# Moving PSUM copies to ScalarE and elementwise steps to GpSimd in an edge-gated graph kernel

## The chip, the cores and the metric

The kernel runs on one core of a Trainium2 chip. A core has a matrix engine (TensorE, "PE" in the profile, with its weight loads under "PEld"), VectorE ("DVE"), ScalarE ("ACT"), GpSimd ("POOL") and a queue engine for transfers (SyncE, "SP"); ScalarE and GpSimd issue transfers too. Working memory is SBUF; matrix products land in PSUM. The metric is the device time of one execution in microseconds, as the median of several. A separate execution was recorded by the hardware profiler.

## The reference

The inputs are `x` of 16 x 1024 x 256 and a sparse adjacency `adj` of 1024 x 1024 (some nine nonzeros in a row). With D = 256, what is computed is

```
pre_u = x @ W1[:D];  pre_v = x @ W1[D:]
hidden[b,u,v] = relu(pre_u[b,u] + pre_v[b,v] + b1)
S[b,u,v] = sigmoid(hidden[b,u,v] @ W2 + b2)
a_t[b,v] = sum_u S[b,u,v] * adj[u,v] * x[b,u]
m_t[b,v] = (sum_u adj[u,v] * x[b,u]) * x[b,v]
z = beta1*x + beta2*(a_t @ Wa + ba) + beta3*(m_t @ Wm + bm)
```

Only the pairs (u, v) with a nonzero `adj[u,v]` matter, so the gate S is needed for edges alone. The output has the shape of `x`, in float32.

## The kernel before, in words

**Tiles.** The 16 batches go in NG = 4 groups of GB = 4, the 1024 target nodes v in NT = 8 tiles of 128. One group and one tile are a block: 32 blocks, numbered k in `order`. A block has two windows w of 64 nodes, and a window has TW = 5 slots j of 128 edges each, so a block is T = 10 steps and the whole kernel 320 steps n = 10k + s. Within a window, the edges in slot j belong to one or two quarters of 16 nodes (`QUARTERS`).

**Edge lists.** `lists(vt)`, a generator driven by the table `advance`, turns a tile of `adjT` into slots: VectorE finds the nonzeros, and `uidx`, `vidx`, `onehot` and `whose` hold, for each edge, its source node, the flat address of its weight, its target within a quarter and within a window. `fetch_val` gathers the weights themselves into `val` with GpSimd transfers, two a step while any are wanted.

**Tables.** `rows` writes h W1[:D] into `table[g]` in DRAM, whose other half is a copy of x (`copy_h`). `fetch(n)` (line 453) has GpSimd gather, for the 128 edges of step n, 128 rows of 8 KB from the table into one of NF = 5 buffers `fetched`.

**The target side.** `halves(k)` makes h W1[D:] + b1 for block k in PSUM (two halves of 128 x 512). ScalarE copies it into `X`, rounded to the matmul's fp32r format (line 418), and VectorE takes the product less `X` as `low`, the rest that rounding lost (line 419). ScalarE then puts `X` and `low` of a window into the two halves of the partitions (lines 422 and 425). Thus one fp32r matmul by a 0/1 matrix `mark` gives the sum of both parts: `expand(n)` (line 523) spreads the 128 nodes' rows over the 128 edges of step n into the PSUM tile `pc` of 128 x 1024, which has two buffers.

**A step.** `gate(n)` adds `fetched` and `pc` on VectorE into `t` in SBUF (line 539), and four `scalar_tensor_tensor` (line 543), one a batch, take the relu, multiply by W2 and sum into `sc`. ScalarE makes the sigmoid (line 546). `left_adj(n)` has already put onehot times the adj weight into the "adj columns" of the tile `left` (line 533, ScalarE); ScalarE multiplies these by the gate into the columns beside them (line 549, four a step). `aggregate(n)` (line 560) multiplies `left` by the gathered x into `acc`, both m and a at once.

**End of a block.** `half_end` copies `acc` to SBUF, `turn_over` transposes it and ScalarE writes it to `LT`; `times_h` (line 591, VectorE) multiplies its m part by h; `block_end` (line 608) multiplies by Wm and Wa into a PSUM tile `pz` that begins with the bias; `add` (line 612, VectorE) adds beta1 h in place in `h_blk`, and SyncE sends `h_blk` out. The last block has a path of its own, `tail`.

**What sets the order.** It is written out by hand: `manual_schedule` keeps each engine's queue in program order. The main loop issues, for each n: aggregate(n-1), up to two weight gathers, fetch(n+4), gate(n), left_adj(n+1), the deferred work of `do(n)`, expand(n+2), and then, at fixed s, pieces of `turn_over`, `block_end`, `halves` and `rows`. `after(step, f)` puts f into `do(step)`. So on GpSimd, fetch(n+4) stands behind the wait for aggregate(n-1), which frees its buffer. PSUM holds two tiles of `pc`, two of `acc`, and two for the small products (`small`, "misc" in the profile).

Of the kernel before, what the change touches and what calls it, by code (L numbers as in the profile page):

```python
# [13 lines left out]
P = 128  # L14
# [3 lines left out]
def kernel(  # L18
# [46 lines left out]
    GB = 4  # L65
# [292 lines left out]
    def after(step, f):  # L358
        due.setdefault(step, []).append(f)
# [48 lines left out]

    def halves(k):
        X = cuts[k] = big.tile([P, NW, GD], FR, name="X")  # L410
        low = one.tile([P, GD], FR, name="low")
        for h in range(2):
            step = yield
            c = slice(2 * h * D, (2 * h + 2) * D)
            p = small("p")
            add_row(p, b1_p)
            half_product(p, hTs[order[k]], w_v, h, True)
            nc.scalar.copy(X[:, 0, c], p)
            after(step + 1, lambda c=c, p=p: nc.vector.tensor_tensor(
                low[:, c], p, X[:, 0, c].bitcast(FP), ALU.subtract))  # L420
        yield
        nc.scalar.copy(X[W:, 1, :], X[W:, 0, :].bitcast(FP))
        for w in range(NW):
            yield
            nc.scalar.copy(X[(1 - w) * W:(2 - w) * W, w, :], low[w * W:(w + 1) * W].bitcast(FP))

    engines = mybir.EngineType
    main.enter_context(tc.manual_schedule(
# [98 lines left out]
    def left_adj(n):  # L527
        k, g, vt, w, j = where(n)
        i = vt * NW + w
        m = len(QUARTERS[j])  # L530
        o = max(2 * j - 1, 0)
        lefts[n] = wk.tile([P, 2, GB, 2, V], FP, name="left")
        nc.scalar.activation(lefts[n][:, :m, :, 0, :], onehot[:, i, o:o + m, :].unsqueeze(2).to_broadcast([P, m, GB, V]),  # L533
                             AF.Copy, scale=val[:, i, j:j + 1])

    def gate(n):
        k, g, vt, w, j = where(n)
        t = one.tile([P, GB, D], FP, name="t")
        nc.vector.tensor_tensor(t, fetched[n % NF][:, :GD].rearrange("p (b d) -> p b d", b=GB),  # L539
                                pcs.pop(n).rearrange("p (b d) -> p b d", b=GB), ALU.add)  # L540
        sc = wk.tile([P, GB], FP, name="sc")
        for b in range(GB):
            nc.vector.scalar_tensor_tensor(t[:, b, :], t[:, b, :], 0.0, w2_b,  # L543
                                           ALU.max, ALU.mult, accum_out=sc[:, b:b + 1])
        gt = wk.tile([P, GB], FP, name="gt")
        nc.scalar.activation(gt, sc, AF.Sigmoid, bias=b2_b)  # L546
        for b in range(GB):
            m = len(QUARTERS[j])
            nc.scalar.activation(lefts[n][:, :m, b, 1, :], lefts[n][:, :m, b, 0, :], AF.Copy, scale=gt[:, b:b + 1])  # L549

    def aggregate(n):
        k, g, vt, w, j = where(n)
        left, f = lefts.pop(n), fetched[n % NF]
        for i, q in enumerate(QUARTERS[j]):
            h, r = divmod(q, 2)
            first = j == h * MID and r == 0
            if first:
                accs[h] = psa.tile([P, 2, D], FP, name=f"acc{h}")
            for b in range(GB):
                nc.tensor.matmul(accs[h][b * 2 * V:(b + 1) * 2 * V, r, :],  # L560
                                 left[:, i, b].rearrange("p k v -> p (k v)"), f[:, GD + b * D:GD + (b + 1) * D],
                                 start=first, stop=(j == q + 1), skip_group_check=True)


# [5 lines left out]
    def turn_over(k, w, q, step):  # L570
# [17 lines left out]

        def times_h():
            m = LT[:, :, :, 0, v]  # L590
            nc.vector.tensor_tensor(m, m, hTs[order[k]].rearrange("p b c n -> p c b n")[:, :, :, v], ALU.mult)  # L591
            if w == NW - 1 and q == 1:
                del hTs[order[k]]
        after(step + 1, times_h)

    def block_end(k):

        g, vt = order[k]
        hb = hbs[k]
        for h in range(2):  # L600
            for bb in range(2):
                step = yield
                if bb == 0:
                    pz = small("pz")
                    add_row(pz, bias_p)
                for i, wt in enumerate((w_m, w_a)):
                    for c in range(DC):
                        nc.tensor.matmul(pz[:, bb * D:(bb + 1) * D], LTs[k][:, c, 2 * h + bb, i, :], wt[:, c, :],  # L608
                                         start=False, stop=(i == 1 and c == DC - 1), skip_group_check=True)

            def add(h=h, pz=pz):
                nc.vector.scalar_tensor_tensor(hb[:, 2 * h:2 * h + 2, :], hb[:, 2 * h:2 * h + 2, :], be1,
                                               pz.rearrange("p (b d) -> p b d", b=2), ALU.mult, ALU.add)
            after(step + 1, add)
        after(step + 2, lambda: nc.sync.dma_start(
            out[g * GB:(g + 1) * GB, vt * P:(vt + 1) * P, :].rearrange("b p d -> p b d"), hb))
        del hbs[k], LTs[k]


# [64 lines left out]
    for n in range(total + 2):  # L684
# [54 lines left out]
        elif n >= total:  # L739
# [1 line left out]
            next(end)  # L741
            go(end, n)
            go(end, n)
        if k + 1 < BS and s in (0, 2, 3, 4, 6):
            if s == 0:
                parts = halves(k + 1)
                next(parts)
# [129 lines left out]
```

## Time and profile before

| What | Value |
|---|---|
| median of 3 runs | 1183.41 us (1183.29 to 1184.95) |
| profiled execution: time, span | 1197.01 us, 1195.2 us |
| PE busy | 1097.9 us, 92% |
| DVE busy | 1066.9 us, 89% |
| ACT busy | 840.4 us, 70% |
| POOL busy | 426.1 us, 36% |
| transfers | 391.39 MB, mean 327 GB/s |
| mean granted TensorE clock | 0.973 |

The span runs from the first to the last instruction of the profiled execution; that execution is 1.1% above the median of the runs. Busy is the time in which an engine works on data; the issuing of a transfer by SP or ACT isn't counted, the gathers that GpSimd makes are. In the lists of groups a row gives line, engine, operation, output and inputs with their shapes, how many there were, and then the busy time in us, the mean time of one in ns, and the idle time of the engine just before them with what ended it. In the chain that ended last the profiler follows only the last microseconds here, so it says little.

### The profile page before, as it was taken

Reading aid. Unit: us, or ns where it says so; the run is one execution under the profiler, and the core shown is the slowest. Engines: PE = TensorE matmul, PEld = TensorE weight load, DVE = VectorE, ACT = ScalarE, POOL = GpSimd, SP = SyncE. Lnnn points to the kernel's source line nnn. Section 1 sums busy time; section 2 is a strip of 40 time slices with the busy share of each in tenths; the row PEclk is TensorE's granted clock in tenths of the full one; section 3 lists DMA queues with packets and bytes.
Section 4 is the critical chain, followed back from the end, with each engine's and each line's share of the span. In section 5 each row is a group of like instructions: output and inputs, shape, how many; then the busy total and the mean of one; then the engine's idle time right before and its main releaser. Section 6 shows DMA issues by size and latency. Waiting matters only on the chain. (4 is left out here: it accounts for less than half of the span.)

```text
span 1195.2 us, 23788 instructions
## 1 busy us (share of the span) xinstructions
PE 1097.9 (92%) x7633; PEld 724.7 (61%) x7633; DVE 1066.9 (89%) x3515; ACT 840.4 (70%) x2498; POOL 426.1 (36%) x428
## 2 busy tenths in 40 slices
PE   7667988999889898999999999999999999999986
PEld 6544655666556565666666666666666666666653
DVE  8769879989988988899899999999999999999994
ACT  3346666677667665777777777787878777777873
POOL 1557652433263226333233333333333333333330
PEclk9968899999999999999999999999999999999998
DMA  9988889899979978999999999999999999999992
GB/s 279 312 307 261 258 319 333 315 336 377 320 254 373 361 244 302 357 384 360 351 329 379 359 331 371 362 356 386 358 367 345 356 324 326 326 341 328 335 340 76
DMA packets 147046, 391.39 MB, mean 327 GB/s; under 512 B 16752, under 2 KB 105328, under 8 KB 110704
## 3 DMA queue, kind: packets, MB, share of 16 engines
q0 software_dynamic: 50016, 300.50, 68.5%
q1 hardware_dynamic: 81616, 74.99, 19.6%
q10 hardware_dynamic: 15280, 14.29, 3.7%
q8 instruction: 63, 1.03, 0.3%
q14 instruction: 71, 0.58, 0.1%
HBM read 393.78 MB, written 50.33 MB: 372 GB/s over the span
## 5 line engine op out<-in xcount | busy, mean ns | idle before, releaser
L453 POOL DMA_INDIRECT fetched<-table,uidx x320 | 329.7, 1030 | 675.5 <-PE acc L560 509.6
L543 DVE SCALAR_TENSOR_TENSOR t<-t,w_b 128x256 f32<-128x256 f32 x1280 | 469.3, 422 | 20.1 <-ACT LT L581 0.5
L539 DVE TENSOR_TENSOR t<-fetched,pc 128x1024 f32<-128x1024 f32 x320 | 388.8, 1215 | 22.4 <-DMA fetched<-table,uidx 8.6
L560 PE MATMUL acc<-fetched,left 128*32 128x256 f32 x4096 | 334.2, 394 | 32.3 <-ACT left L549 16.8
L549 ACT ACTIVATE left<-left,gt 128x32 f32<-128x32 f32 (+1 forms) x1280 | 299.4, 304 | 10.4
L523 PE MATMUL pc<-X,mark 128*128 128x512 f32 x640 | 238.1, 454 | 21.1 <-DVE t L539 13.6
L560 PEld LDWEIGHTS acc<-fetched,left 128*32 128x32 f32 x4096 | 129.9, 110 | 177.2 <-issue 46.9
L546 ACT ACTIVATE gt<-sc,b_b 128x4 f32<-128x4 f32 x320 | 95.3, 298 | 140.5 <-DVE t L543 133.9
L523 PEld LDWEIGHTS pc<-X,mark 128*128 128x128 f32 x640 | 97.2, 191 | 156.6 <-issue 102.2
L608 PE MATMUL misc<-w_a,LT 128*128 128x256 f32 x496 | 127.3, 379 | 0.0
L608 PE MATMUL misc<-w_m,LT 128*128 128x256 f32 x496 | 127.1, 378 | 0.0
L384 PE MATMUL misc<-w_u,hT 128*128 128x256 f32 x448 | 109.2, 390 | 11.0 <-ACT few L298 3.6
L533 ACT ACTIVATE left<-onehot,val 128x128 f32<-128x128 bf16 (+1 forms) x320 | 116.5, 364 | 0.0
L384 PE MATMUL misc<-w_v,hT 128*128 128x256 f32 x448 | 107.9, 384 | 0.0
L543 DVE DVE_READ_ACCUMULATOR t<-t,w_b 128x1 f32 x1280 | 104.2, 81 | 0.0
L608 PEld LDWEIGHTS misc<-w_m,LT 128*128 128x128 f32 x496 | 93.7, 189 | 17.2
L384 PEld LDWEIGHTS misc<-w_u,hT 128*128 128x128 f32 x448 | 85.8, 195 | 27.3 <-issue 4.4
L608 PEld LDWEIGHTS misc<-w_a,LT 128*128 128x128 f32 x496 | 94.2, 190 | 12.8
L568 ACT COPY ev<-acc 128x512 f32<-128x512 f32 x128 | 75.1, 587 | 34.7 <-PE acc L560 26.8
L341 POOL DMA_INDIRECT val<-in_adjT_dram,vidx x80 | 83.6, 1046 | 33.4 <-issue 21.9
L384 PEld LDWEIGHTS misc<-w_v,hT 128*128 128x128 f32 x448 | 86.7, 194 | 14.3
L581 ACT COPY LT<-misc 128x512 f32<-128x512 f32 x128 | 71.1, 575 | 24.0 <-PE pc L523 12.0
(158 smaller groups left out, 830.9 us busy)
## 6 DMA issues: line engine op xcount, KB each, us to landing
h_blk<-in_x_dram SPq DMA_DIRECT2D x31, 512.0 KB
out_dram<-h_blk SPq DMA_DIRECT2D x31, 512.0 KB
hT<-in_xT_dram SPq DMA_DIRECT2D x28, 512.0 KB
table<-tab SPq DMA_DIRECT2D x26, 512.0 KB
table<-in_x_dram ACTq DMA_DIRECT2D x24, 512.0 KB
fetched<-table,uidx POOLq DMA_INDIRECT x320
table<-in_x_dram SPq DMA_DIRECT2D x8, 512.0 KB
table<-fetched SPq DMA_DIRECT2D x6, 512.0 KB
```

The source lines that it names most:

```text
L341: nc.gpsimd.indirect_dma_start(out=val[:, i, j:j + 1], out_offset=None, in_=adj_flat, in_offset=bass.IndirectOffsetOnAxis(ap=vidx[:, i, j: ...
L384: nc.tensor.matmul(p[:, bb * D:(bb + 1) * D], hT[:, 2 * h + bb, i, :], wt[:, i, :], start=(i == 0 and not begun), stop=(i == DC - 1), skip ...
L453: nc.gpsimd.indirect_dma_start(out=fetched[n % NF], out_offset=None, in_=table[g], in_offset=bass.IndirectOffsetOnAxis(ap=uidx[:, vt * NW ...
L523: nc.tensor.matmul(pcs[n][:, c], marks[n // TW][:, j * P:(j + 1) * P], cuts[k][:, w, c], start=True, stop=True)
L533: nc.scalar.activation(lefts[n][:, :m, :, 0, :], onehot[:, i, o:o + m, :].unsqueeze(2).to_broadcast([P, m, GB, V]), AF.Copy, scale=val[:, ...
L539: nc.vector.tensor_tensor(t, fetched[n % NF][:, :GD].rearrange("p (b d) -> p b d", b=GB), pcs.pop(n).rearrange("p (b d) -> p b d", b=GB), ...
L543: nc.vector.scalar_tensor_tensor(t[:, b, :], t[:, b, :], 0.0, w2_b, ALU.max, ALU.mult, accum_out=sc[:, b:b + 1])
L546: nc.scalar.activation(gt, sc, AF.Sigmoid, bias=b2_b)
L549: nc.scalar.activation(lefts[n][:, :m, b, 1, :], lefts[n][:, :m, b, 0, :], AF.Copy, scale=gt[:, b:b + 1])
L560: nc.tensor.matmul(accs[h][b * 2 * V:(b + 1) * 2 * V, r, :], left[:, i, b].rearrange("p k v -> p (k v)"), f[:, GD + b * D:GD + (b + 1) * D ...
L568: nc.scalar.copy(evs[q], accs.pop(q))
L608: nc.tensor.matmul(pz[:, bb * D:(bb + 1) * D], LTs[k][:, c, 2 * h + bb, i, :], wt[:, c, :], start=False, stop=(i == 1 and c == DC - 1), sk ...
```

## The change

Four edits go together.

1. In `halves` both PSUM products are copied out by ScalarE: a second copy puts the product itself into `low` (now float32), and the subtraction works on SBUF alone, in place. It runs on GpSimd, except for block 0.
2. `left_adj` and `times_h` go to GpSimd (`times_h` of the last block stays on VectorE).
3. In `block_end` ScalarE copies `pz` to a new tile `z`, right after the products; GpSimd multiplies `h_blk` by beta1 in place and adds it to `z`; SyncE sends `z` out. The product by Wa comes before that by Wm.
4. `gate` has no tile `t` any more: the sum of `fetched` and `pc` is written back into `pc` in PSUM, and the four relu-and-sum instructions read and write it there.

The fourth piece of `halves` (the first copy out of `low`) moves from s = 4 to s = 5.

```diff
-        low = one.tile([P, GD], FR, name="low")
+        low = one.tile([P, GD], FP, name="low")
+        engine = nc.gpsimd if k else nc.vector
...
             nc.scalar.copy(X[:, 0, c], p)
-            after(step + 1, lambda c=c, p=p: nc.vector.tensor_tensor(
-                low[:, c], p, X[:, 0, c].bitcast(FP), ALU.subtract))
+            nc.scalar.copy(low[:, c], p)
+            after(step + 1, lambda c=c: engine.tensor_tensor(low[:, c], low[:, c], X[:, 0, c].bitcast(FP), ALU.subtract))
...
-        nc.scalar.activation(lefts[n][:, :m, :, 0, :], onehot[:, i, o:o + m, :].unsqueeze(2).to_broadcast([P, m, GB, V]),
-                             AF.Copy, scale=val[:, i, j:j + 1])
+        nc.gpsimd.tensor_scalar(lefts[n][:, :m, :, 0, :], onehot[:, i, o:o + m, :].unsqueeze(2).to_broadcast([P, m, GB, V]),
+                                val[:, i, j:j + 1], None, ALU.mult)
...
-        t = one.tile([P, GB, D], FP, name="t")
-        nc.vector.tensor_tensor(t, fetched[n % NF][:, :GD].rearrange("p (b d) -> p b d", b=GB),
-                                pcs.pop(n).rearrange("p (b d) -> p b d", b=GB), ALU.add)
+        t = pcs.pop(n).rearrange("p (b d) -> p b d", b=GB)
+        nc.vector.tensor_tensor(t, fetched[n % NF][:, :GD].rearrange("p (b d) -> p b d", b=GB), t, ALU.add)
...
-            nc.vector.tensor_tensor(m, m, hTs[order[k]].rearrange("p b c n -> p c b n")[:, :, :, v], ALU.mult)
+            (nc.vector if k == BS - 1 else nc.gpsimd).tensor_tensor(m, m, hTs[order[k]].rearrange("p b c n -> p c b n")[:, :, :, v], ALU.mult)
...
+        z = big.tile([P, GB, D], FP, name="z", bufs=1)
...
-                for i, wt in enumerate((w_m, w_a)):
+                for i, wt in ((1, w_a), (0, w_m)):
...
-            def add(h=h, pz=pz):
-                nc.vector.scalar_tensor_tensor(hb[:, 2 * h:2 * h + 2, :], hb[:, 2 * h:2 * h + 2, :], be1,
-                                               pz.rearrange("p (b d) -> p b d", b=2), ALU.mult, ALU.add)
+            sl = slice(2 * h, 2 * h + 2)
+            nc.scalar.copy(z[:, sl], pz.rearrange("p (b d) -> p b d", b=2))
+
+            def add(sl=sl):
+                nc.gpsimd.tensor_scalar(hb[:, sl], hb[:, sl], be1, None, ALU.mult)
+                nc.gpsimd.tensor_tensor(z[:, sl], hb[:, sl], z[:, sl], ALU.add)
             after(step + 1, add)
...
-            out[g * GB:(g + 1) * GB, vt * P:(vt + 1) * P, :].rearrange("b p d -> p b d"), hb))
+            out[g * GB:(g + 1) * GB, vt * P:(vt + 1) * P, :].rearrange("b p d -> p b d"), z))
...
-        if k + 1 < BS and s in (0, 2, 3, 4, 6):
+        if k + 1 < BS and s in (0, 2, 3, 5, 6):
```

## The prediction

> **What bounds the kernel now.** I began with the page's busy times, and with how they lie over the span (busy by stretches; the columns are PE, PEld, DVE, ACT, POOL, granted clock, DMA share, GB/s).
>
> ```profile
> PE 1097.9 (92%) x7633; PEld 724.7 (61%) x7633; DVE 1066.9 (89%) x3515; ACT 840.4 (70%) x2498; POOL 426.1 (36%) x428
> 300.00:360.00 60.00, 50.84 (x349) 32.50 (x350) 54.62 (x183) 39.11 (x121) 26.60 (x26) 0.97 0.86 289
> 840.00:900.00 60.00, 59.77 (x430) 39.65 (x426) 55.83 (x175) 47.20 (x143) 19.54 (x19) 1.00 1.01 366
> 1080.00:1140.00 60.00, 57.70 (x410) 36.81 (x410) 58.13 (x184) 46.94 (x146) 19.76 (x20) 1.00 0.93 331
> ```
>
> The limits differ. Late, DVE is busy 58 of 60 us and DMA 0.93; in the middle DMA is full (1.01) and PE nearly; early nothing is full, so engines wait for each other. Which of PE and DVE leads is told by the timeline of two late steps:
>
> ```profile
> 1005.41 1.22 DVE L539 TENSOR_TENSOR t<-fetched,pc 128x1024 f32<-128x1024 f32 x1
> 1006.67 0.42 DVE L543 SCALAR_TENSOR_TENSOR t<-t,w_b 128x256 f32<-128x256 f32 x1
> ...
> 1008.06 0.74 DVE L612 SCALAR_TENSOR_TENSOR h_blk<-h_blk,be,misc 128x512 f32<-128x512 f32 x1
> 1008.72 1.21 DVE L539 TENSOR_TENSOR t<-fetched,pc 128x1024 f32<-128x1024 f32 x1
> 1011.59 1.22 DVE L539 TENSOR_TENSOR t<-fetched,pc 128x1024 f32<-128x1024 f32 x1
> ```
>
> DVE goes from gate to gate with no gap. By the starts of L539, a step with the gate alone takes 2.81 us, and one with an L419, L591 or L612 besides 3.2 to 3.4. Blocks 24 to 30 take 31.1 us each: 10 x 2.81 and 3.0 for the six extras. The groups with shapes kept apart give the pieces:
>
> ```profile
> L453 POOL DMA_INDIRECT fetched<-table,uidx x320 | 329.7, 1030 | 675.5 <-PE acc L560 509.6 <-DVE t L543 52.0 <-DVE h_blk L612 44.8
> L533 ACT ACTIVATE left<-onehot,val 128x128 f32<-128x128 bf16 x192 | 74.0, 386 | 0.0
> L612 DVE SCALAR_TENSOR_TENSOR h_blk<-h_blk,be,misc 128x512 f32<-128x512 f32 x62 | 46.1, 744 | 20.7 <-PE misc L608 20.6
> L419 DVE TENSOR_TENSOR low<-misc,X 128x512 fp32r<-128x512 f32 x64 | 43.9, 686 | 19.7 <-ACT X L418 19.7
> L591 DVE TENSOR_TENSOR LT<-LT,hT 128x512 f32<-128x512 f32 x55 | 37.8, 688 | 11.1 <-ACT LT L581 10.9
> L418 ACT CAST X<-misc 128x512 fp32r<-128x512 f32 x64 | 37.3, 583 | 38.4 <-PE misc L384 32.4 <-PE pc L523 4.0 <-PE misc L578 1.6
> ```
>
> The three DVE rows that leave also carry 51.5 us of waits at the head of DVE's queue, with the next gate behind them; 37 us of these lie before 540 us.
>
> By the starts of L539 I cut the span into prologue (68.5 us), early blocks 0 to 10 (431.6), middle 11 to 22 (395.5), late 23 to 31 (278.6) and tail (21.0): 1195.2 us. The execution took 1197.0, 13.6 above the median of the runs; I take the same difference for the change.
>
> [...] L419 (PSUM) takes 686 ns, L591 (SBUF) 688.
>
> **The change part by part, per block of ten steps.**
>
> *DVE.* Two each of L612, L419 and L591 leave: 3.0 us. The gate keeps its instructions. Writing PSUM isn't in the trace; by the read rows it costs nothing[...]. I take 20 ns on the four L543s: 0.8 a block. DVE then needs 28.9 us, against 31.1.
>
> *PE* keeps its work, but expand(n+2) must now wait for the last L543 of gate(n), not for L539, some 1.4 us later. Read off the timeline where PE doesn't wait: expand 0.57 to the next start, aggregate 0.57 or 1.0 (one or two quarters), Wa and Wm products 7.4 a block, `halves` 3.9, transposes 2.0: 5.7 + 8.3 + 7.4 + 3.9 + 2.0 = 27.3 us, and 3.5 more in a block with `rows` (nine in ten in the middle), 30.5. Expand finishes 0.57 us after gate(n), and is needed after gate(n+1), 2.8 us later. So PE may lag DVE by 2.2; in steps 2 to 6 its work (16.3 us) exceeds DVE's (14.1) by just that. I cost the new wait at nothing, hidden by gate(n+1); without that cover it is up to 0.57 + 1.4 us a step. Wa ahead of Wm gives the later `times_h` 0.9 us more.
>
> *ACT* loses L533 (3.6 us) and gets four 128x512 copies (4 x 0.58): 1.3 us less. Each waits for PE at the head of its queue, where L418 waited already; the sigmoid stands behind. It has 70% load: nothing.
>
> *POOL* is where the work goes. A gather is 0.99 us and starts 1.30 apart when nothing holds it: 13.0 us. No elementwise row of POOL with these shapes exists. [...] L533's successor: [...] 0.39 by ACT's row, a gather's 0.99 as high end; I take 0.5. Sum: 10 x 0.5 + 6 x 1.2 + 2 x 0.85 = 13.9, so 26.9 us a block: 90% of what is left. The fetch of n+4 and left(n+1) stand behind `add` or `times_h`, and ACT's L549, then aggregate(n+1), behind left(n+1). Cover: aggregate(n+1) comes 5.4 us after aggregate(n-1) on PE; 1.3 + 0.5 + 1.0 (L549) + 0.9 are used, so 1.7 us of queueing is free. `add` (2.05) barely is. Gathers have four steps of lead.
>
> In val steps POOL issues three gathers: 3.9 + 0.5 + up to 2.05. Steps 1 to 15 all have two vals: 15 x 4.4 + 9.3 = 75 us on POOL against 65.4 spent there now, +10. [...] The one swap in this trace, at 471.0 us, shows nothing of the sort. I add nothing for it[...].
>
> *DMA* moves the same bytes from `z` instead of `h_blk`. `z` has one buffer: SP sends it at s = 8, and ACT's next copy into it comes at s = 4, six steps or 18 us later, so that wait is covered; were the transfer slower, the sigmoids would stand behind the copy. At share 0.93 and 31.1 us, late blocks can't go below 28.9; the middle (0.96 to 1.01 in its stretches, 33.0 a block) barely below 32.2.
>
> **Sum.** Late: DVE 28.9, DMA 28.9, PE 27.3, POOL 26.9, and four limits so close don't mesh perfectly: I take 29.5, -1.6 x 9 = -14. Middle: DMA decides, -0.8 x 12 = -10. Early: 37 us of waits and 33 us of DVE work leave, of which PE, DMA (0.82 to 0.97) and POOL leave a third, -23; vals +10, later vals +3: -10. Prologue and tail keep their VectorE work; the two copies more of block 0 (1.2 us of ACT) lie before the first gather lands: nothing. Altogether -34: 1161 us of span, 1149 us as a median.
>
> **Rivals.** *PSUM is dear*: [...] late 0, middle -3, early -8: 1172 us. [...] L419 against it. *GpSimd becomes the bound*, the slower side: elementwise at 1.5 times my prices makes 33.9 us of POOL a block, gathers come late behind it, and with them aggregate. Late 9 x 2.8 = +25, middle 12 x 0.9 = +11, early -5: +31, 1214 us. It decides from about 19.5 us of elementwise a block (1.4 times), where late blocks lose what the others gain. For it speaks that these prices are no rows of this trace; against it POOL's 675 us of idle before gathers. *Everything meshes*: DMA can be squeezed to 1.0 throughout, its 92% of the span leaving -60: 1123 us. That the edits don't do what they say is excluded by the queues: the three rows leave DVE.
>
> **How the numbers follow.** Likeliest 0.53 (1132 to 1168), PSUM dear 0.17, GpSimd the bound 0.22, meshing 0.08. A measurement of this kernel can't tell less than about 0.2% from no change. Faster: 0.53 + 0.08 + 0.13 of the dear case, 0.74; same 0.05; slower 0.21. The range from 1118 to 1208 leaves out the worse half of the GpSimd case and the best of meshing.
>
> **What would show it.** Steps of the gate alone stay at 2.8 to 2.9 us, late blocks come at 29 to 30; L543's successor keeps 422 ns; POOL is at 70 to 85% with left at 0.5 us; waits of DVE turn to `pc` or `fetched`; blocks 0 and 1 are longer. Wrong: L543 at 490 ns or more, ACT's L549 or PE's aggregate waiting for POOL's left for tens of us, or steps above 3.3 us throughout.

## The result and the profile after

The changed kernel takes 1320.22 us (median of 4 runs, 1315.39 to 1326.26), against 1183.35 for the kernel before on the same chip: a ratio of 1.1157, 95% interval 1.1104 to 1.1211. The forecast was 1149 us, with a range up to 1208. It is slower by 137 us, where 34 us of gain were expected.

The profiled execution has a span of 1315.6 us. Cut by the starts of the gate's first instruction, as the forecast cut it, the loss lies here (us; forecast and measured change in the last columns):

| Stage | before | after | forecast | measured |
|---|---|---|---|---|
| prologue | 68.5 | 72.0 | 0 | +3.5 |
| early, blocks 0 to 10 | 431.5 | 505.6 | -10 | +74.1 |
| middle, blocks 11 to 22 | 395.6 | 417.5 | -10 | +21.9 |
| late, blocks 23 to 31 | 278.6 | 299.3 | -14 | +20.7 |
| tail | 21.0 | 21.1 | 0 | +0.1 |

These add up to +120 us and not to +137, because the profiled execution of the kernel before lay 13.6 us above its median and that of the kernel after 2.8 us below. So wherever stages are set beside those of the kernel before, the losses come out somewhat small.

Busy times of the page, and busy time by stretches (columns PE, PEld, DVE, ACT, POOL, granted clock, DMA share, GB/s), of the kernel after:

```profile
PE 1128.9 (86%) x7633; PEld 744.5 (57%) x7633; DVE 1110.4 (84%) x3329; ACT 811.8 (62%) x2304; POOL 944.6 (72%) x996
```

```profile
480.00:540.00 60.00, 46.27 (x275) 30.15 (x275) 45.67 (x131) 28.29 (x82) 36.89 (x38) 0.91 0.68 225
1140.00:1200.00 60.00, 55.30 (x398) 34.78 (x391) 56.01 (x164) 42.70 (x124) 48.69 (x51) 1.00 0.87 307
```

VectorE has 186 instructions fewer and yet 43.5 us more busy time. Late it is busy for 56.0 of 60 us with 164 instructions, where the kernel before got 184 into 58.1; DMA has fallen from 0.93 to 0.87. Around 500 us every engine is idle for nearly a fourth of the time or more. So there are two troubles: a VectorE that does less in the same time, and, early, engines that wait for each other. The clock granted to TensorE is also lower early (0.91 in the early stage, 0.95 before); in the middle and late it is 1.00 in both kernels. What part of the early loss belongs to it wasn't tested.

The first is read off the timeline of VectorE in a late step (start, duration, engine, line, operation, operands), kernel after:

```profile
1167.98 1.26 DVE L542 TENSOR_TENSOR pc<-fetched,pc 128x1024 f32<-128x1024 f32 x1
1169.35 0.43 DVE L545 SCALAR_TENSOR_TENSOR pc<-pc,w_b 128x256 f32<-128x256 f32 x1
1169.70 0.14 DVE L545 DVE_READ_ACCUMULATOR pc<-pc,w_b 128x1 f32 x1
1169.87 0.43 DVE L545 SCALAR_TENSOR_TENSOR pc<-pc,w_b 128x256 f32<-128x256 f32 x1
...
1171.27 1.26 DVE L542 TENSOR_TENSOR pc<-fetched,pc 128x1024 f32<-128x1024 f32 x1
```

The sums still take 0.43 us, but come 0.52 us apart (1169.35, 1169.87). Each consists of the sum and of an instruction that reads its accumulator; here the next sum starts when that read has ended (1169.70 + 0.14 = 1169.84). In the kernel before the next sum and the accumulator read start together, and sums come 0.35 us apart (1006.67, 1007.02); behind the first of these sums, kernel before:

```profile
1007.02 0.08 DVE L543 DVE_READ_ACCUMULATOR t<-t,w_b 128x1 f32 x1
1007.02 0.42 DVE L543 SCALAR_TENSOR_TENSOR t<-t,w_b 128x256 f32<-128x256 f32 x1
```

The semaphores that the trace keeps with each instruction say why. In the kernel after, every accumulator read raises VectorE's own semaphore, and the second to fourth sum of every step (960 of 960) wait for it. In the kernel before none of the 960 does, although there, too, each sum writes its elements over what it has read: the tile `t`, in SBUF. So it isn't writing in place that makes the chain, but writing in place in a PSUM tile. Why the program gets such waits for the four separate slices of a PSUM tile, and none for those of an SBUF tile, no run here shows.

A step with the gate alone takes 3.29 us (1167.98 to 1171.27); it took 2.81. And 3.30 is now the median of all late steps: ten of them are 33.0 us, and blocks 24 to 30 take 33.0 to 34.1 us each. Late, the chain sets the pace of the steps. The groups by shape show how little of it is in the durations, kernel before (two rows) and after:

```profile
L543 DVE SCALAR_TENSOR_TENSOR t<-t,w_b 128x256 f32<-128x256 f32 x1280 | 469.3, 422 | 20.1 <-ACT LT L581 0.5
L543 DVE DVE_READ_ACCUMULATOR t<-t,w_b 128x1 f32 x1280 | 104.2, 81 | 0.0
```

```profile
L545 DVE SCALAR_TENSOR_TENSOR pc<-pc,w_b 128x256 f32<-128x256 f32 x1280 | 553.5, 432 | 65.7 <-ACT X L426 0.5
L545 DVE DVE_READ_ACCUMULATOR pc<-pc,w_b 128x1 f32 x1280 | 180.9, 141 | 0.0
L542 DVE TENSOR_TENSOR pc<-fetched,pc 128x1024 f32<-128x1024 f32 x320 | 400.4, 1251 | 101.1 <-DMA fetched<-table,uidx 60.6 <-PE pc L524 38.1 <-PE misc L610 1.7
L534 POOL TENSOR_SCALAR left<-onehot,val 128x128 f32<-128x128 bf16 x192 | 119.9, 625 | 17.2 <-issue 8.9
L617 POOL TENSOR_SCALAR h_blk<-h_blk,be 128x512 f32<-128x512 f32 x62 | 96.8, 1561 | 0.0
L421 POOL TENSOR_TENSOR low<-low,X 128x512 f32<-128x512 f32 x62 | 79.0, 1275 | 0.0
```

A sum has gone from 422 to 432 ns, the addition from 1215 to 1251, the accumulator read from 81 to 141. Below stand GpSimd's own prices.

The second trouble is in the list of waits (in us: total, times, longest), kernel after:

```profile
ACT left L550 <- POOL left L534: 113.4, 64, 16.7
PE pc L524 <- DVE pc L545: 73.0, 66, 4.0
```

ScalarE waits 113.4 us for the adj columns that GpSimd now writes, 103.1 of them before 578 us, and TensorE's expand waits 73.0 us for VectorE's last sum. The longest single wait, 16.7 us, is step 104, which takes 18.49 us. GpSimd's timeline there, kernel after (in brackets the idle time before):

```profile
532.68 0.63 POOL L534 TENSOR_SCALAR left<-onehot,val 128x128 f32<-128x128 bf16 x1
540.90 0.39 POOL L766 PARTITION_ALL_REDUCE longest<-rest  x1 [7.58 <-DVE pc L545]
541.49 1.25 POOL L454 DMA_INDIRECT fetched<-table,uidx  x1 [0.20 <-issue]
551.67 0.61 POOL L534 TENSOR_SCALAR left<-onehot,val 128x128 f32<-128x128 bf16 x1 [8.93 <-issue]
```

This is the one all-reduce over partitions of the kernel. GpSimd stands still for 7.58 us before it and for 8.93 us before the next elementwise instruction. In the kernel before, which had no elementwise work around it, the idle time before it was 0.20 us.

The profile puts the first pause down to a sum of VectorE, but GpSimd's own records show something nearer. Where GpSimd goes from elementwise work to the all-reduce, or back, the trace has a pair of MODIFY_POOL_CONFIG records. Such a pair is what the forecast and the expectations call a swap, and what it sets, which no trace shows, a library. The first pair at this all-reduce, kernel after (count, duration in ns, first and last start in us):

```profile
L766 POOLq MODIFY_POOL_CONFIG  x2: 28/30/32, 533.3 to 533.3; - x2
```

It comes 7.6 us before the all-reduce; the second pair, at 542.8 us, 8.8 us before the next `left`. The first `left` of the kernel has a pair as well, but starts 0.14 us behind it, and so does the all-reduce of the kernel before (0.13 us). Block 10, which holds this step, takes 62.0 us for 35.6: 26 of the early stage's 74 us.

### The profile page after: what moved, and what is told of

Same layout as the page of the kernel before. It is cut to its first block, busy times and chain, and to the rows that moved or that the text cites. A ratio compares the mean times of both kernels' runs of the same rounds, so it can differ in the third digit from the quotient of the medians.

```text
span 1315.6 us, 24802 instructions
## 1 busy us (share of the span) xinstructions
PE 1128.9 (86%) x7633; PEld 744.5 (57%) x7633; DVE 1110.4 (84%) x3329; ACT 811.8 (62%) x2304; POOL 944.6 (72%) x996
## 4 chain that ended last, share of the span: by engine, by line
DVE 30%; PE 28%; POOL 12%; DMA 12%; issue 12%; ACT 4%; POOLq 0%; DVEq 0%; ACTq 0%
DVE pc L545 16%; DMA fetched<-table,uidx 11%; DVE pc L542 9%; PE misc L384 7%; PE acc L561 6%; PE pc L524 5%; PE misc L610 5%; POOL fetched L454 5%; POOL left L534 3%; POOL h_blk L617 2%; ACT left L550 1%; POOL val L341 1%; POOL low L421 1%; PE misc L388 1%; PE misc L579 1%
## 5 line engine op out<-in xcount | busy, mean ns | idle before, releaser
L545 DVE SCALAR_TENSOR_TENSOR pc<-pc,w_b 128x256 f32<-128x256 f32 x1280 | 553.5, 432 | 65.7 <-ACT X L426 0.5
L454 POOL DMA_INDIRECT fetched<-table,uidx x320 | 341.0, 1066 | 256.6 <-PE acc L561 167.0
L542 DVE TENSOR_TENSOR pc<-fetched,pc 128x1024 f32<-128x1024 f32 x320 | 400.4, 1251 | 101.1 <-DMA fetched<-table,uidx 60.6
L561 PE MATMUL acc<-fetched,left 128*32 128x256 f32 x4096 | 352.5, 397 | 66.9 <-ACT left L550 66.4
L550 ACT ACTIVATE left<-left,gt 128x32 f32<-128x32 f32 (+1 forms) x1280 | 299.6, 304 | 138.6 <-POOL left L534 113.4
L561 PEld LDWEIGHTS acc<-fetched,left 128*32 128x32 f32 x4096 | 139.4, 110 | 218.2 <-ACT left L550 96.4
L534 POOL TENSOR_SCALAR left<-onehot,val 128x128 f32<-128x128 bf16 (+1 forms) x320 | 179.5, 561 | 23.2 <-issue 9.3
L545 DVE DVE_READ_ACCUMULATOR pc<-pc,w_b 128x1 f32 x1280 | 180.9, 141 | 0.0
L384 PE MATMUL misc<-w_v,hT 128*128 128x256 f32 x448 | 114.4, 402 | 0.0
L384 PEld LDWEIGHTS misc<-w_v,hT 128*128 128x128 f32 x448 | 92.2, 206 | 16.7
L617 POOL TENSOR_SCALAR h_blk<-h_blk,be 128x512 f32<-128x512 f32 x62 | 96.8, 1561 | 0.0
L419 ACT CAST X<-misc 128x512 fp32r<-128x512 f32 x64 | 37.4, 584 | 90.6 <-PE misc L384 90.6
```

The source lines that it names most:

```text
L384: nc.tensor.matmul(p[:, bb * D:(bb + 1) * D], hT[:, 2 * h + bb, i, :], wt[:, i, :], start=(i == 0 and not begun), stop=(i == DC - 1), skip ...
L454: nc.gpsimd.indirect_dma_start(out=fetched[n % NF], out_offset=None, in_=table[g], in_offset=bass.IndirectOffsetOnAxis(ap=uidx[:, vt * NW ...
L534: nc.gpsimd.tensor_scalar(lefts[n][:, :m, :, 0, :], onehot[:, i, o:o + m, :].unsqueeze(2).to_broadcast([P, m, GB, V]), val[:, i, j:j + 1], ...
L561: nc.tensor.matmul(accs[h][b * 2 * V:(b + 1) * 2 * V, r, :], left[:, i, b].rearrange("p k v -> p (k v)"), f[:, GD + b * D:GD + (b + 1) * D ...
L617: nc.gpsimd.tensor_scalar(hb[:, sl], hb[:, sl], be1, None, ALU.mult)
```

## The experiments

Four theories were put on record. GATE WAITS: the in-place sums wait for one another. PSUM PRICE: VectorE's access to PSUM is slow in itself. GPSIMD: its new work delays gathers and `left`, and so ScalarE and TensorE. LONG HOLD: `pc` is held until the last sum has ended, so TensorE's expand comes late. Each ratio is to the kernel before, on the same chip, with its 95% interval. The chips differ: the kernel before took 1181 to 1184 us on some and 1202 to 1204 on others, where one of the changed kernels took the same 1284 us on both kinds. So ratios from chips of different kinds aren't compared closer than 2%; the ledger at the end puts the main terms on one chip.

**The gate edit alone.** The kernel before with the sum in place in PSUM:

```diff
-        t = one.tile([P, GB, D], FP, name="t")
-        nc.vector.tensor_tensor(t, fetched[n % NF][:, :GD]..., pcs.pop(n)..., ALU.add)
+        t = pcs.pop(n).rearrange("p (b d) -> p b d", b=GB)
+        nc.vector.tensor_tensor(t, fetched[n % NF][:, :GD]..., t, ALU.add)
```

> The kernel before, with the in-place sum in PSUM alone; all else stays with its engine. Three theories. GATE WAITS: each of the four sums that writes back into pc waits for the one before it, so that a step costs 3.3 us in place of 2.8; here late blocks come at 35 to 36 us (10 x 3.27 + 3.0 for the six extras, which are still on VectorE), the median at 1290 to 1330. PSUM PRICE: the same time, but because each access to PSUM is dearer; the distance between two sums is then longer also where no wait lies between them. GPSIMD: the sum in PSUM costs little, the loss is GpSimd's; the median stays at 1183 to 1200 and steps with the gate alone at 2.8 to 2.9 us.

Measured: 1352.98 us against 1201.61, ratio 1.126 (1.1219 to 1.1302). This edit alone costs no less than the whole change, and more than was expected. Sums come 0.53 us apart, each behind a wait for the one before (960 of 960); late blocks take mostly 36.3 us, since VectorE still has the rows that the whole change takes from it. The other edits, put on top of it, gain in the late blocks (325.3 to 299.3 us) and in the middle (443.8 to 417.5) and lose in the early ones (490.9 to 505.6). A group of this kernel:

```profile
L523 PE MATMUL pc<-X,mark 128*128 128x512 f32 x640 | 236.1, 451 | 212.4 <-DVE pc L542 182.6 <-DVE cut L254 6.5 <-ACT mark L516 5.0
```

TensorE's expand waits 182.6 us for VectorE's last sum.

**Which part of the edit?** The same kernel, with the sums reading `pc`, but leaving their unused products in `fetched`, in SBUF:

```diff
+        o = fetched[n % NF][:, :GD].rearrange("p (b d) -> p b d", b=GB)
-            nc.vector.scalar_tensor_tensor(t[:, b, :], t[:, b, :], 0.0, w2_b,
+            nc.vector.scalar_tensor_tensor(o[:, b, :], t[:, b, :], 0.0, w2_b,
```

> The kernel before, with the sum of gathered rows and pc in place in PSUM and the four relu-and-sum instructions reading it there, while their elementwise result goes over the gathered rows in SBUF. GATE WAITS: with no write back into pc no sum waits for the one before it: 0.35 us apart, steps of the gate alone 2.7 to 2.8 us, late blocks 30 to 31.5 us, median within 2% of the kernel before, although expand still waits for the last sum. PSUM PRICE: steps of 3.1 to 3.3 us, median 6 to 12% above. LONG HOLD of pc (expand waits for the last sum and PE can't work ahead): sums 0.35 us apart, but PE's waits for them and the median 3 to 8% above.

Measured: 1229.15 us against 1182.20, ratio 1.0393 (1.0376 to 1.0411). Sums are 0.35 us apart again, none waits for the one before it, and they take as long from PSUM as they did from SBUF. Group and wait of this kernel:

```profile
L543 DVE SCALAR_TENSOR_TENSOR fetched<-pc,w_b 128x256 f32<-128x256 f32 x1280 | 466.7, 421 | 20.1 <-DVE pc L539 0.5
```

```profile
PE pc L523 <- DVE fetched L543: 106.7, 95, 3.4
```

So PSUM PRICE falls for reads (421 against 422 ns), and the writes of the sums into PSUM cost some 1.126 - 1.039 = 8.7% of the time (from two chips of different kinds; by the medians 10%), by the spacing and not by their duration. A step with the gate alone takes 2.63 us, less than the 2.81 of the kernel before, and still the kernel is 3.9% slower. What is left is the wait of expand: 106.7 us.

**The hold by itself.** The kernel before, in which only the fourth sum touches `pc`, by writing its unused product there:

```diff
-            nc.vector.scalar_tensor_tensor(t[:, b, :], t[:, b, :], 0.0, w2_b,
+            nc.vector.scalar_tensor_tensor((pc if b == GB - 1 else t)[:, b, :], t[:, b, :], 0.0, w2_b,
```

> The kernel before, with one thing more: the fourth relu-and-sum instruction puts its elementwise result (which nobody reads) into pc in place of t, so that expand must wait for the last sum of the gate before it may refill that buffer; the gate is otherwise as before. LONG HOLD: PE can't work ahead in the steps that have block_end or halves; the median lies 3 to 6% above the kernel before, PE waits for VectorE's sums before expand by about 100 us, and steps 5 and 0 of a late block take 3.5 to 4 us. If the 4% of the run with the sums in SBUF came from PSUM accesses instead, the median stays within 1% of the kernel before.

Measured: 1247.93 us against 1203.61, ratio 1.0337 (1.0291 to 1.0383). The wait and the groups of this kernel:

```profile
PE pc L523 <- DVE pc L544: 106.7, 100, 3.5
```

```profile
L544 DVE SCALAR_TENSOR_TENSOR t<-t,w_b 128x256 f32<-128x256 f32 x960 | 358.4, 422 | 20.1 <-DVE t L540 0.5
L544 DVE SCALAR_TENSOR_TENSOR pc<-t,w_b 128x256 f32<-128x256 f32 x320 | 136.7, 427 | 0.0
...
L544 DVE DVE_READ_ACCUMULATOR t<-t,w_b 128x1 f32 x960 | 78.4, 82 | 0.0
L544 DVE DVE_READ_ACCUMULATOR pc<-t,w_b 128x1 f32 x320 | 44.8, 140 | 0.0
```

The late step with the gate alone is 2.86 us, 0.05 over the kernel before, and the same 106.7 us of waiting appear. LONG HOLD stands, with some 3 to 4%, through TensorE. The rows add a detail: the same sum that writes to PSUM takes 5 ns more, and its accumulator read 58 ns more.

**No `t`, no hold.** The kernel before, with the gate in place over `fetched` in SBUF:

```diff
-        t = one.tile([P, GB, D], FP, name="t")
-        nc.vector.tensor_tensor(t, fetched[n % NF][:, :GD]..., pcs.pop(n)..., ALU.add)
+        t = fetched[n % NF][:, :GD].rearrange("p (b d) -> p b d", b=GB)
+        nc.vector.tensor_tensor(t, t, pcs.pop(n)..., ALU.add)
```

> The kernel before, with the sum written in place over the gathered rows in SBUF: pc is free after the sum, as before, no sum waits for another, and the next gate needn't wait until t has been read. Steps with the gate alone then take 2.65 us in place of 2.81, late blocks 29.4 to 30 us in place of 31.1, the middle hardly changes since transfers are full there; median 0.97 to 0.99 of the kernel before. If VectorE doesn't set the pace, 1.00.

Measured: 1204.00 us against 1203.61, ratio 0.9992 (0.9969 to 1.0016), no difference. Steps with the gate alone fall to 2.64 us, but late blocks stay at 30.6 to 32.1: other steps grow longer, s = 0 above all (2.8 to 4.3 us, for 2.82). Busy time by stretches of this kernel, late:

```profile
1020.00:1080.00 60.00, 58.37 (x424) 37.27 (x421) 58.38 (x186) 48.40 (x148) 20.61 (x20) 1.00 0.94 336
```

VectorE and TensorE are both at 58.4 of 60 us. The forecast read a VectorE "with no gap" as the one limit; 0.17 us a step taken from it brought nothing. Here, too, the sums write in place over a tile, in SBUF, and none of the 960 waits for the one before: they stay 0.35 us apart. Which instruction of TensorE paces such a block wasn't followed.

**The changed kernel with its gate mended.** First, in the changed kernel, the edit with `o` of above: sums read PSUM and write SBUF.

> The changed kernel, with the sum of gathered rows and pc still in place in PSUM and the four relu-and-sum instructions still reading it there, but their elementwise result (which nobody reads) put over the gathered rows in SBUF. GATE WAITS: no instruction waits for the one before it, sums 0.35 us apart, median as with the sum in SBUF, 1240 to 1270. PSUM PRICE: sums stay 0.5 us apart or at least 0.42, median 1290 to 1320. GPSIMD: 1305 to 1325.

Measured: 1284.25 us against 1201.61, ratio 1.0714 (1.0669 to 1.076). The spacing is that of GATE WAITS, 0.35 us; the time lies between those put down for it and for PSUM PRICE. Group of the gate's addition in this kernel:

```profile
L542 DVE TENSOR_TENSOR pc<-fetched,pc 128x1024 f32<-128x1024 f32 x320 | 392.7, 1227 | 240.7 <-DMA fetched<-table,uidx 162.1 <-PE pc L524 63.7 <-PE acc L562 11.1
```

VectorE now waits 162.1 us for gathers, where it waited 60.6: with the gate's chain gone, other waits take its place. The late stage falls only from 299.3 to 292.4 us. Second, the changed kernel with the gate in place over `fetched`, as in the diff before:

> The changed kernel, with the sum written in place over the gathered rows in SBUF instead of over pc in PSUM; the rest of the change stays. GATE WAITS and PSUM PRICE: sums 0.35 us apart again, steps from 3.3 towards 2.9, bounded then by GpSimd with its 30 us a block; median 1240 to 1270, late blocks 30 to 32 us. GPSIMD: nothing is gained, 1305 to 1325, late blocks still 33 us, with VectorE idle. If VectorE and GpSimd get into each other's way (two SBUF inputs), sums are above 422 ns or GpSimd's rows longer than 1.28 us.

Measured: 1315.15 us against 1201.61, ratio 1.096 (1.0927 to 1.0993). There is neither hold nor chain here, yet it is slower than with the sums from PSUM into SBUF; the time is the one put down for GPSIMD. Two groups of this kernel show another price:

```profile
L545 DVE SCALAR_TENSOR_TENSOR fetched<-fetched,w_b 128x256 f32<-128x256 f32 x1280 | 658.2, 567 | 33.2 <-ACT left L550 0.5
...
L617 POOL TENSOR_SCALAR h_blk<-h_blk,be 128x512 f32<-128x512 f32 x62 | 112.4, 1813 | 0.0
```

With both inputs in SBUF a sum takes 567 ns instead of 422, and GpSimd's instruction 1813 instead of 1561. With `t` in PSUM the sums have one SBUF input, and take 422 ns (sums into SBUF) or 432 (in place) beside the same work of GpSimd.

**Adj columns back on ScalarE**, in the changed kernel:

```diff
-        nc.gpsimd.tensor_scalar(lefts[n][:, :m, :, 0, :], onehot..., val[:, i, j:j + 1], None, ALU.mult)
+        nc.scalar.activation(lefts[n][:, :m, :, 0, :], onehot..., AF.Copy, scale=val[:, i, j:j + 1])
```

> The changed kernel with the adj columns back on ScalarE; the gate stays in PSUM. GPSIMD: 5.6 us a block leave GpSimd and the 113 us of ScalarE's waits for it go; median 1220 to 1250. GATE WAITS: late and middle blocks stay at 33 us since VectorE paces them, only the early blocks gain, 30 to 50 us; median 1270 to 1290. The stall of 18.5 us at step 104 gets shorter or goes in both[...].

Measured: 1301.35 us against 1201.61, ratio 1.0826 (1.0783 to 1.087). The early blocks take 490.5 us, for 505.6, less than either theory gave; late steps stay at 3.30 us, as GATE WAITS had it. With the sums into SBUF as well:

> The changed kernel with two parts undone: adj columns on ScalarE, and the elementwise results of the sums in SBUF (the sum itself stays in PSUM). GATE WAITS and GPSIMD are then both out: late blocks 28.5 to 30 us (VectorE needs 28), middle 32 to 33[...]; median 0.99 to 1.02 of the kernel before. If only one of the two mattered, it lands at that one's time alone: 1.07 with the sums, 1.08 with the columns.

Measured: 1253.16 us against 1182.20, ratio 1.0599 (1.0572 to 1.0626), well above what was expected. The hold is still in it, 3.9% by itself on this chip. With `left` on ScalarE and the gate over `fetched`:

> The changed kernel, with the adj columns on ScalarE and the sum in place over the gathered rows in SBUF: what is left of the change are ScalarE's copies out of PSUM and GpSimd's low, times_h and add. LONG HOLD and GATE WAITS are both out. If the moved parts help once these are gone: late blocks 28 to 30 us, median 0.97 to 1.00. If GpSimd's work and its clash with VectorE (two SBUF inputs) cost more than VectorE saves: 1.02 to 1.06, sums above 422 ns in the mean, and VectorE waiting for gathers.

Measured: 1295.73 us against 1203.61, ratio 1.0726 (1.0659 to 1.0794). Sums take 570 ns, so `left` was not what clashed with them. It is worse than the worse of the two forecasts.

**The pause at the all-reduce.** The kernel with `left` on ScalarE and the sums into SBUF, with the all-reduce put off to the end, so that no elementwise instruction follows it:

```diff
-        if n == 100:
+        if n == total - 1:
...
-            after(n + 12, count_rest)
+            after(total + 2, count_rest)
```

> As the one before, with the all-partitions maximum, and the two small copies behind it, moved from steps 100 and 112 to the last step[...]. If the stall near step 104 is the library, 12 to 18 us less than the run before it, and no wait of 9 us on GpSimd near 550 us; if it is the wait for the edge lists, no change there.

Measured: 1247.56 us, ratio 1.0558 (1.0512 to 1.0603), against 1.0599 on the same chip: 0.4 points, which the intervals don't tell apart. Block 10 falls from 58.9 to 41.5 us, but block 0 goes from 44.8 to 52.5, the tail from 21.1 to 25.5 and the prologue from 69.1 to 72.2. In block 0 GpSimd has 9.71 us of idle time before its first `low`, which took 0.37 before. So the pause has moved rather than gone. The trace has a pair of MODIFY_POOL_CONFIG records here too, 9.6 us before that first `low`, and another at the end, 5.7 us before the all-reduce. In all 18 profiles a pair is followed by a pause (5.7 to 9.6 us) just where the work behind it, elementwise or all-reduce, is of another kind than that behind the pair before it, if the first pair of an execution is counted as coming after the last of the execution before; the others cost 0.14 us or less. That anything stays from one execution to the next is inferred from this pattern, not tested by itself. It would explain why putting the all-reduce last doesn't get rid of the pause: the next execution pays for it.

**Moves alone, with the gate as before.** First only the adj columns on GpSimd (the diff of `left_adj`, reversed):

> The kernel before, with one of the moves alone: GpSimd writes the adj columns of left; the gate keeps its tile t in SBUF, and all else is as before. GPSIMD theory: from after, undoing this move gave 3.3% and, once the sums were no longer chained, 1.1%; alone it should cost 0.5 to 2%, with the loss in early blocks (two swaps with the collective after block 9, and GpSimd steps with three gathers), ScalarE waiting for left over 60 us in all, late blocks as before (31.1 us). The step (e) and (f) of the prediction, which added some 10 us for this and nothing for the swap: 0.3 to 1%. A late loss of over 1 us a block would speak for a delay of ScalarE's products in every step.

Measured: 1233.00 us against 1181.33, ratio 1.0454 (1.0405 to 1.0502), over twice the most that was expected. The place of the loss was right: late blocks take 31.3 to 31.9 us (31.1 before), the early ones +33 us in all, and block 10 alone 55.7 against 35.6, with one step of 17.32 us at the all-reduce. Waits and group of this kernel:

```profile
ACT left L549 <- POOL left L533: 64.4, 30, 15.7
PE acc L560 <- ACT left L549: 63.5, 62, 12.4
```

```profile
L533 POOL TENSOR_SCALAR left<-onehot,val 128x128 f32<-128x128 bf16 x192 | 153.7, 800 | 18.0 <-issue 8.9 <-PE acc L560 0.8
```

ScalarE's wait for `left` stands beside one of TensorE's aggregate of the same size. And `left` takes 800 ns here, 625 after; that fits the clash in SBUF, since here the gate has sums with two SBUF inputs beside it.

Last, `low` and `times_h` on GpSimd with ScalarE's copies, the end of the block and the gate as before. In the whole change `z` and `t` do not both fit in SBUF, so `add` was left where it was:

```diff
             nc.scalar.copy(X[:, 0, c], p)
+            nc.scalar.copy(low[:, c], p)
-            after(step + 1, lambda c=c, p=p: nc.vector.tensor_tensor(low[:, c], p, ...
+            after(step + 1, lambda c=c: engine.tensor_tensor(low[:, c], low[:, c], ...
...
-            nc.vector.tensor_tensor(m, m, hTs[order[k]]...
+            (nc.vector if k == BS - 1 else nc.gpsimd).tensor_tensor(m, m, hTs[order[k]]...
```

> The kernel before, with the products of halves copied out of PSUM by ScalarE and the subtraction for low and times_h on GpSimd; adj columns on ScalarE, the gate with t in SBUF and block_end as before. The prediction's mechanism (VectorE's rows and the waits in front of it leave, 2.0 us a late block): late blocks 29.5 to 30.5 us, 1 to 2% faster. GPSIMD theory: the same work off VectorE meets PE as the next limit and GpSimd's two-input steps of 1.28 us come behind gathers: 0.5% faster to 1% slower, late blocks 30.6 to 31.4. If L543 with two SBUF inputs rises above 450 ns, it is the clash of VectorE and GpSimd in SBUF that takes the gain, and the kernel is 1 to 3% slower.

Measured: 1247.60 us, ratio 1.0571 (1.0525 to 1.0618); late blocks mostly 33.5 us, 2.4 longer, although two each of the 686 and 688 ns instructions of VectorE, 2.7 us, left each of them. What was put down last, the clash in SBUF, shows, at a greater cost than the 1 to 3% named there. Group of the sums, and the timeline of a late step that takes 5.31 us instead of 3.24, in this kernel:

```profile
L546 DVE SCALAR_TENSOR_TENSOR t<-t,w_b 128x256 f32<-128x256 f32 x1280 | 572.7, 502 | 33.8 <-ACT left L534 0.9 <-ACT left L551 0.5
```

```profile
1068.50 1.28 POOL L421 TENSOR_TENSOR low<-low,X 128x512 f32<-128x512 f32 x1
...
1069.03 1.04 DVE L546 SCALAR_TENSOR_TENSOR t<-t,w_b 128x256 f32<-128x256 f32 x1
...
1070.70 2.21 DVE L546 SCALAR_TENSOR_TENSOR t<-t,w_b 128x256 f32<-128x256 f32 x1
...
1071.35 1.27 POOL L593 TENSOR_TENSOR LT<-LT,hT 128x512 f32<-128x512 f32 x1
```

Two sums of 0.42 us take 1.04 and 2.21. Both end 0.29 us after GpSimd's instruction: at 1070.07 after 1068.50 + 1.28 = 1069.78, and at 1072.91 after 1071.35 + 1.27 = 1072.62. So a sum isn't slowed in proportion; it stands until the other instruction is through. The two lose 0.62 + 1.79 = 2.41 us, which is what this step has over the 2.89 of its neighbours. The second stood still before GpSimd's recorded start; starts of GpSimd in the profile are rough. All 113 sums of this kernel that take over 0.5 us end 0.29 us after a `low` or `times_h` of GpSimd, of which there are 124, and together they lose 103 us. Of the early loss, block 10 with the all-reduce has 16.3 us (51.9, for 35.6). What ScalarE's copies cost by themselves wasn't run.

**The ledger.** Four kernels on one chip, each with one term more than that above it: the hold (sums read `pc`, write `fetched`), then `low`, `times_h` and `add` moved, then `left` moved, then the sums written in place, which is the whole change. No new edits are in them.

> The kernel before, its sum in place in PSUM and the four sums reading it there, their products left in SBUF: the hold of pc alone. LONG HOLD: 3.4 to 4% over before.

> The same gate, and besides low, times_h and add on GpSimd with ScalarE's copies; adj columns on ScalarE. If the costs of the parts add, this is 5.7% or more over the kernel with the hold alone, what the move of low and times_h cost beside a gate in SBUF; if the gate's reading from PSUM protects it from GpSimd, 1.5 to 2.5%.

> The same, and the adj columns on GpSimd too. By the ratios of the separate chips 1.1% over the kernel with the moves alone, by their medians 2.5%, by the move alone on the kernel before 4.5%. Since the pause at the all-reduce is paid already, the GPSIMD theory expects 1 to 2.5%.

> The whole change: the same with the products of the sums written in place. If the waits between the sums cost what they cost alone (8.7%), 1.16 to before; if steps that wait for GpSimd hide part of them, 1.10 to 1.12, 3 to 4.5% over the kernel without these writes.

Measured, with stages cut as above (us):

| Kernel | median | ratio (95%) | early | middle | late |
|---|---|---|---|---|---|
| before | 1182.71 | 1 | 431.5 | 395.6 | 278.6 |
| + hold | 1230.89 | 1.0402 (1.0385 to 1.0420) | 443.4 | 409.5 | 287.7 |
| + low, times_h, add | 1251.37 | 1.0582 (1.0556 to 1.0608) | 464.3 | 406.3 | 287.1 |
| + left | 1283.94 | 1.0846 (1.0828 to 1.0864) | 485.2 | 412.0 | 293.5 |
| + sums in place (all) | 1326.01 | 1.1235 (1.1207 to 1.1263) | 503.2 | 420.8 | 300.6 |

(The stages of the kernel before are those of its first profile.) The steps are 4.0, 1.8, 2.6 and 3.9 points; the third and the total come slightly above what was put down for them. In this order the moves of `low`, `times_h` and `add` cost 1.8 points where those of `low` and `times_h` alone cost 5.7 beside a gate in SBUF, and the writes in place 3.9 where the gate's edit by itself had given 8.7. Parts hide each other, so the ledger is one order of several. The two moves cost their time mostly early (+21 us each), `left` also some 6 us in the middle and late; hold and writes cost it throughout.

Two readings of these profiles go further. The early 21 us of `low`, `times_h` and `add` lie at the pause: block 10 grows from 35.6 to 58.6 us, the other early blocks together fall by 2.0. Those of `left` don't: it adds only 2.0 us to block 10. And late they take 30 us of work off VectorE (267.7 to 237.8 us busy), while the stage stays (287.7 to 287.1): with the hold in place, VectorE's work isn't what the late blocks wait for.

## Why the prediction was wrong, by its own steps

**"I cost the new wait at nothing, hidden by gate(n+1)": failed.** Expand's wait for the last sum costs 3.4 to 4.0% by itself (`pc` written by one sum, or read by four), with 106 to 107 us of waiting in TensorE's queue in each case. The working gave TensorE a lag of 2.2 us, and found that steps 2 to 6 use just that, so nothing was left for any step that isn't the mean. The loss lies at s = 5 (3.81 us in late blocks, for 3.31), s = 3 (3.55, for 3.24) and s = 0 (3.3 to 4.2, for 2.82), in or after the steps in which TensorE has `halves` and `block_end`; that it is these pieces which expand used to run ahead of is argued, not shown.

**"I take 20 ns on the four L543s": failed, and what it left out sets the pace late.** The 20 ns were the author's estimate; the duration was near (10 ns more). The cost is between the instructions: every sum in the PSUM tile waits for the one before, with its accumulator read of 141 ns, and spacing goes from 0.35 to 0.52 us. A step grows by 0.48 us: what the forecast put down was a price for accesses, and the cost was an order. By the ledger it is 3.9 points; 8.7 with the gate's edit alone. Late steps come 3.30 us apart for the 2.95 of the forecast's 29.5 us a block, 31 of the 35 us by which the late stage is above its forecast. But that isn't what the chain is worth there, for without it the stage shortens by 7 us only (300.6 to 293.5 in the ledger). Writing over the tile just read was not new, since the kernel before did it in `t`; new was that the tile lies in PSUM, and the waits that the program then has between the sums.

**"PSUM is dear"**: the rival of 1172 us had the place and not the mechanism. The sums read PSUM at no cost (421 ns, and 422 from SBUF), as L419 against L591 had said (686 and 688), and writing it cost 5 to 10 ns on a sum. The price on which the rival's 1172 us rest is shown by no trace or run.

**GpSimd's sum: mis-sized.** Per block: 16.4 us measured for 13.9. The two-input instruction took 1.28 us for 1.2, `left` 0.56 for 0.5; the 128x512 tensor_scalar 1.56 for 0.85. The 1.2 and the 0.85 were the author's estimates, with no row of the trace before behind them. The 16.4 us are less than the 19.5 from which the rival was to decide, and late it doesn't: GpSimd has 48.7 of 60 us there, and moving its work on top of the gate's edit gained. Once the chain is gone, `left` costs 6 us late. As a rival it had the wrong place: it put its loss in late and middle blocks and a gain in the early ones.

**"Vals +10"; "I add nothing for it" (the swap): failed.** The pauses are 7.58 and 8.93 us at step 104, each behind a pair of MODIFY_POOL_CONFIG records, and block 10 is 16 to 23 us longer in three kernels that move only a part onto GpSimd (51.9, 55.7 and 58.9 us against 35.6). The estimate was read from the one all-reduce of the kernel before (0.20 us of idle time before it), which had no elementwise work to come back to. Besides, ScalarE waits 103.1 us early for `left` (the pause's 16.7 among them), which stands behind GpSimd's gathers, so "1.7 us of queueing is free" didn't hold there.

**"37 us of waits and 33 us of DVE work leave": a third was to come back, and none did.** With the gate in SBUF, the moved instructions hold up the sums (502 ns in the mean, for 422). With the gate in PSUM, the chain paces the steps; without the chain the hold is left, and 30 us less of VectorE work late brought 0.6 us. No kernel that was run moves the rows without one of the three.

**What held.** The three rows left VectorE and ScalarE lost little (ACT 811.8 us for 840.4). L543's successor, which was to keep 422 ns, took 432 in PSUM beside GpSimd's work; with the gate in SBUF it took 567. The signs that were put down as showing it wrong appeared: ScalarE waiting for `left`, and steps at 3.30 us throughout. The L543 of 490 ns didn't.

**What stays open**: what paces the late blocks when the gate is shortened; why only sums in a PSUM tile are made to wait; what the lower clock takes early; what a pair of MODIFY_POOL_CONFIG records sets, and whether that stays from one execution to the next. None of the kernels that were run is faster than the one before.

## What to carry to other kernels

When results are written back into a PSUM tile, look at what the instruction behind must now wait for (in place in PSUM 960 of 960 sums waited here, in SBUF none), and at what the tile's later release keeps waiting on another engine: durations show neither, the spacing of starts and the waits of the tile's next writer do. Before moving elementwise work to GpSimd, ask which VectorE instructions with two SBUF inputs run beside it (sums of 502 and 567 ns here, for 422), what on GpSimd's queue stands behind it, and whether an all-reduce comes between (pauses of 7.6 and 8.9 us here). Costs found part by part don't add: here three edits cost 12.6, 4.5 and 5.7% alone, and the whole change 11.6%.

## What the runs showed of the hardware

- An accumulator read after a sum that writes its elements to PSUM took 140 to 141 ns in the mean, after one to SBUF 78 to 84.
- VectorE's sums of 128x256 read PSUM as fast as SBUF (421 and 422 ns) and write it 5 to 10 ns slower.
- VectorE sums with two SBUF inputs that met GpSimd instructions of 1.28 and 1.27 us took 1.04 and 2.21 us instead of 0.42; all 113 long ones of that kernel ended 0.29 us after a GpSimd instruction. GpSimd's instructions are longer beside such sums as well: 1813 instead of 1561 ns, 800 instead of 625.
- On GpSimd a one-input 128x512 tensor_scalar with a per-partition factor (1.56 us) took longer than a two-input tensor_tensor (1.28 us).
- With elementwise work before and after an all-reduce over partitions, GpSimd stood still for 7.6 and 8.9 us, each time behind a pair of MODIFY_POOL_CONFIG records; in all 18 profiles such a pair was followed by 5.7 to 9.6 us or by 0.14 us or less, in the pattern told above.
